# Two changes to the order of issue in a selective-scan and spectral-convolution kernel: decays two scans ahead, product copies 500 columns later

## The chip, the cores and the metric

The kernel runs on one core of one Trainium2 chip. The metric is the device time of one execution in microseconds. Five engines work side by side, each through its own queue in order: TensorE (PE in the profile, its weight loads PEld), VectorE (DVE), ScalarE (ACT), GpSimd (POOL) and SyncE (SP), which here only issues DMAs. They meet through semaphores.

## The reference

The input is a batch of four images of 48 × 48 tokens with 128 channels. Layer 0 is a selective scan over the image in four directions, layer 1 self-attention and then a spectral convolution:

```python
# layer 0: group norm, projection, 3x3 depthwise convolution, SiLU; then for 4 directions k
x_dbl = einsum('bkdl,kcd->bkcl', xs, x_proj_w)          # -> dts_r, B, C
dt = softplus(einsum('bkrl,kdr->bkdl', dts_r, dt_proj_w) + dt_proj_b)
h = h * exp(dt_l[..., None] * A) + (dt_l * u_l)[..., None] * B_l   # 2304 steps, 256 x 16 states
y = einsum('bkdn,bkn->bkd', h, C_l)
# the four directions are added, normed, gated and projected; x = x + that
# layer 1: t = t + softmax(ln(t) ln(t)^T) ln(t)
# then, with u = ln(t), for prefixes of 1, 1/2, 1/4 and 1/8 of the tokens:
U_plus  = causal convolution of u with 16 filters
U_minus = the same with alternating signs
out = einsum('btkd,k,kde->bte', U_plus, s, Mpp) + einsum('btkd,k,kde->bte', U_minus, s, Mpm)
out = out + three shifted products of u with M_u
# t = t + weighted sum of the four prefixes' outputs
```

All is computed in float32.

## The kernel before, in words

Each image goes through a prologue (norm, projection, convolution), the scans, an epilogue with attention, and the spectral convolution, which the code calls `stu`. The scans of image b share their time with other work for TensorE: for image 0 with the mixing of the filter matrices (`mixture`), for images 1 to 3 with the `stu` of image b − 1. The `stu` of the last image runs alone at the end.

**The scans.** A chunk is one direction and 384 tokens; there are 24 chunks an image. A chunk has 8 units (two halves of the channels by four groups of states), and a unit four scans, so an image has 768 scans. For each unit VectorE, or GpSimd for three units in eight, multiplies dt·u by B (L451, `enter`); for each scan ScalarE computes the decay exp(dt·A) (L458) into one of three PSUM banks `dAs`, and VectorE runs the scan (L461). GpSimd multiplies the states by C (L470) and keeps the last state (`carry`, L469), TensorE adds over the states (L478), and VectorE adds the result to the image's sum (L484). The first decay of a unit is preceded by a small copy of the carried state into the unit's first column (L456).

**The other ScalarE work of these stages.** `spread` copies a row of B into a PSUM bank for VectorE's multiply (L443). The preparation of a later chunk, cut into small steps by `prepare`, copies projections out of PSUM (L375, L385) and computes a Softplus (L393)[...].

**The Toeplitz products.** `stu` walks through 80 items an image: five blocks of output columns, four of them 126 wide and the last 72, by 16 filters. Each item has three products c = 0, 2, 1 of shifted filters with u (L992), then two projections (L1051, L1055) for the item two before it. The product c = 0 is copied to a second bank (L1006, cy from cx); c = 2 adds to the first bank and c = 1 to the second; both are then copied to `U` (L1011 and L1012, L1009). Each bank has one buffer. A copy isn't issued right behind its product: `later` puts it on a list, and it is issued once so many columns of later matmuls have been issued:

```python
        def later(f):
            late.append([LATER, f])
```

Only the first entry of the list is counted down (`do_late`), and a matmul of a block of width w has two columns for each of its output tokens: 252 or so in the wide blocks, 144 in the last.

**The order.** It is written out by hand and each engine follows it. For every unit s, `scans` goes through enter, a step of preparation, scan 0, a share of TensorE's other work (`more`), the multiply by C of the unit before, scan 1, the addition of a finished y, a step of preparation, `more`, `spread` for unit s + 2, scan 2, `more`, a step of preparation, scan 3, the loads of B and C for the next chunk, the sum over states of unit s − 2, and `more`. `more` takes from the other work so many matmuls that both pieces of work end together; the copies it is due are issued on ScalarE in the same place. In this order a scan's decay is issued immediately ahead of its scan.

SP issues the loads of filters (tt), chunk inputs (rep, bc) and small matrices (G) in the same written order.

Of the kernel before, what the change touches and what calls it, by code (L numbers as in the profile page):

```python
# [24 lines left out]
G4, DL, C4, Q4 = 4, 32, 4, 4  # L25
# [10 lines left out]

BLOCKS = [(0, 126, 0, 72), (126, 252, 1, 18), (252, 378, 2, 36), (378, 504, 3, 0), (504, 576, 3, 0)]
SHIFT = 55.0
LATER = 300


class Stage:
# [13 lines left out]
def hybrid_kernel(ctx: ExitStack, tc: tile.TileContext, a: dict, out: bass.AP):  # L56
# [375 lines left out]
    class Unit:  # L432
# [17 lines left out]
            eng = nc.gpsimd if self.pool else nc.vector  # L450
            eng.tensor_tensor(s, self.ch.rep[self.h][:, :, 1], bt.unsqueeze(1).to_broadcast([P, G4, CS]), ALU.mult)  # L451

        def scan(self, g, i, dAs):
            ch = self.ch
            if g == 0:
                nc.scalar.copy(self.full[:, :, ch.slot], none if ch.first else carry[:, self.h, self.q])  # L456
            dA = dAs[(G4 * i + g) % len(dAs)]
            nc.scalar.activation(dA[:, 1:CS + 1], ch.rep[self.h][:, g, 0], AF.Exp,  # L458
                                 scale=A[:, ch.k, self.h * G4 + g, self.q:self.q + 1])
            s = self.full.rearrange("p g t -> p (g t)")[:, ch.scanned(g)]  # L460
            nc.vector.tensor_tensor_scan(s, dA[:, CS + 1:0:-1] if ch.rev else dA[:, :CS + 1], s, 0.0,  # L461
                                         ALU.mult, ALU.add)
# [49 lines left out]
    def scans(b, chunks, preps, front, sp, back, work, work_cols):  # L512

        units = [Unit(ch, h, q) for ch in chunks for h, q in quads]
        total = len(chunks) * CHUNK_COLS + work_cols
        done = [0]

        def more(share):

            while done[0] < share * total:  # L520
                cols = next(work, None)
                if cols is None:
                    break
                done[0] += cols

        def enter(s):

            if s + 2 < len(units) and units[s + 2].pool:
                units[s + 2].enter(sp.s)
            if 0 <= s + 1 < len(units) and not units[s + 1].pool:  # L530
                units[s + 1].enter(sp.s)

        def spread(s):
            if s < len(units) and not units[s].pool:
                units[s].spread(back.psB)

        def prepare(s):

            ci, j = divmod(s, len(quads))
            for c in range(ci + 1, ci + 4):  # L540
                if c < len(chunks) and 0 <= s - len(quads) * c + LEAD < STEPS:
                    done[0] += next(preps[c]) or 0

        def refill(s, i):

            if 0 <= s < len(units) and s // len(quads) + 1 < len(chunks):
                u, nxt = units[s], chunks[s // len(quads) + 1]
                if u.h == NH - 1:
                    nxt.fetch(i + u.q, front)

        pending = []
        dAs = [back.psa.tile([P, 512], F32, tag=f"dA{i}", name=f"dA{b}_{i}") for i in range(3)]
        for t in dAs:
            nc.vector.memset(t[:, 0:CS + 2:CS + 1], 0.0)
        spread(0)
        enter(-2)
        enter(-1)
        spread(1)
        for s in range(len(units) + 2):
            real = s < len(units)  # L560
            enter(s)
            prepare(s)
            if real:
                units[s].scan(0, s, dAs)
            more((s + 0.25) / len(units))
            if 1 <= s <= len(units):
                units[s - 1].times_c()
            if real:
                units[s].scan(1, s, dAs)
            if pending:  # L570
                pending.pop().add_y()
            prepare(s)
            more((s + 0.5) / len(units))
            spread(s + 2)
            if real:
                units[s].scan(2, s, dAs)
            more((s + 0.75) / len(units))
            prepare(s)
            if real:
                units[s].scan(3, s, dAs)  # L580
            refill(s - 3, Q4)
            refill(s + 1, 0)
            if s >= 2:
                units[s - 2].sum_c(back.psy)
                done[0] += CS
                if units[s - 2].q == Q4 - 1:
                    pending.append(units[s - 2])
            more((s + 1) / len(units))
        for u in pending:
            u.add_y()  # L590
        assert next(work, None) is None
# [308 lines left out]
    def stu(b, pool, ps, seeds):  # L900
# [22 lines left out]
        def do_late(cols=None):  # L923

            if cols is not None and late:
                late[0][0] -= cols
            while late and (cols is None or late[0][0] <= 0):
                late.pop(0)[1]()

        def later(f):  # L930
            late.append([LATER, f])

# [39 lines left out]
        def conv(n, c):  # L972

            assert seq.pop(0) == (n, c)
            (lo, hi, place, extra), k = items[n]
            w = hi - lo
            v = w + (c != 1)
            t = tts[n, c]
            if c == 0:
                banks[0] = ps.psc.tile([P, 512], F32, tag="x", name=f"cx{b}_{n}")  # L980
            elif 1 not in banks:
                do_late()
            p = banks.pop(1) if c == 1 else banks[0]
            p4 = p[:, :4 * v].rearrange("p (e m) -> p e m", e=4)
            nb = (hi + P - 1) // P
            for g in range(2):
                first = lo - (g == 1 and c != 1)
                for J in range(nb):
                    at = max(first, J * P) if J else first
                    end = J * P - 1  # L990
                    x = (sums[:, J, g], u[:, J, 2 + g], u[:, J, g])[c]
                    nc.tensor.matmul(p4[:, 2 * g:2 * g + 2, v - (hi - at):], x,  # L992
                                     t[:, :, hi - 1 - at + J * P:end if end >= 0 else None:-1],
                                     start=(c == 0 and J == 0 and g == 0), stop=(J == nb - 1 and g == 1),
                                     skip_group_check=(c > 0))
                    do_late(2 * (hi - at))
                    if g == 1 and J == nb - 1:
                        later(lambda: taken(n, c, p, w))
                    yield 2 * (hi - at)

        def taken(n, c, p, w):
            if c == 0:
                U[n] = pool.three.tile([P, 8 * P], F32, tag="U", name=f"U{b}_{n}")[:, :8 * w].rearrange(
                    "p (c g e m) -> p c g e m", c=2, g=2, e=2)
                banks[1] = ps.psc.tile([P, 512], F32, tag="y", name=f"cy{b}_{n}")
                nc.scalar.copy(banks[1][:, :4 * w].rearrange("p (e m) -> p e m", e=4),  # L1006
                               p[:, :4 * (w + 1)].rearrange("p (e m) -> p e m", e=4)[:, :, 1:])
            elif c == 1:
                nc.scalar.copy(U[n][:, 0].rearrange("p g e m -> p (g e m)"), p[:, :4 * w])  # L1009
            else:  # L1010
                nc.scalar.copy(U[n][:, 1, 0], p[:, :2 * (w + 1)].rearrange("p (e m) -> p e m", e=2)[:, :, 1:])  # L1011
                nc.scalar.copy(U[n][:, 1, 1].rearrange("p e m -> p (e m)"), p[:, 2 * w + 3:4 * w + 3])  # L1012
# [71 lines left out]
        for n, (_, k) in enumerate(items):  # L1084
            if k == 0:
                begin(n)
            yield from conv(n, 0)
            fetch()
            if n > 0:
                fetch_G(n - 1)  # L1090
            if n > 1:
                if k == 2:
                    yield from ar(n - 2)
                yield from project(n - 2)
            for c in (2, 1):
                yield from conv(n, c)
                fetch()
            if n > 1 and k == 1:
                do_late()
                yield from end(n - 2)  # L1100
# [50 lines left out]
    for b in range(B):  # L1151
# [3 lines left out]
        if b == 0:  # L1155
            mixed = Stage(tc, "m", "right", two=(2, SB))
            scans(b, *first, front, sp, ps, mixture(mixed, ps), MIX_COLS)
            mixed.close()
        else:
            scans(b, *first, front, sp, ps, stu_alone(b - 1, ps, 1), STU_COLS)  # L1160
# [99 lines left out]
```

## Time and profile before

| | |
|---|---|
| median of 3 runs | 6137.34 us (6124.15 to 6143.45) |
| profiled execution | 6131.63 us |
| its span | 6129.9 us |
| PE busy, share | 5042.3 us, 82% |
| PE weight loads | 3316.1 us, 54% |
| DVE | 4264.0 us, 70% |
| ACT | 3258.1 us, 53% |
| POOL | 3630.6 us, 59% |
| scans L461 | 3072, 942 ns each |
| decays L458 | 3072, 584 ns each |
| copies L1011 | 320, 349 ns each |

An engine is busy while it computes; time in which it waits for a semaphore is not counted, and where the profile can tell, it names the instruction that ended the wait, the releaser. TensorE's matmuls are pipelined and their ends are modelled, so its busy time is less sharp than that of the others. The times of single rows come from this one execution. The chain of waits that ended last is made of PE 43%, DVE 25%, DMA 11% and ACT 10%.

### The profile page before, as it was taken

The page shows a single profiled execution, that of the slowest core. Times are in us where ns is not written, and L with a number is a line of the kernel's source. Part 1 is how long each engine was busy: PE and PEld are TensorE (multiplying, and loading weights), DVE is VectorE, ACT ScalarE, POOL GpSimd, SP SyncE. Part 2 cuts the span into 40 slices and gives each one's busy share as a digit, 9 for nine tenths or more (in the row PEclk, how much of TensorE's full clock was granted, in tenths as well). Part 3 has the DMA queues.
Part 4 walks back from the last instruction along what each step waited for, and adds up shares of the span by engine and source line. Part 5 has one row for each costly group of instructions (what it writes and reads, how often), then busy time and mean ns, then how long its engine had stood idle before and what let it go on. Part 6 is the DMA issues. An engine that isn't in the chain of part 4 may idle for free.

```text
span 6129.9 us, 76036 instructions
## 1 busy us (share of the span) xinstructions
PE 5042.3 (82%) x24850; PEld 3316.1 (54%) x24850; DVE 4264.0 (70%) x4926; ACT 3258.1 (53%) x6909; POOL 3630.6 (59%) x1823
## 2 busy tenths in 40 slices
PE   3555555797889988788889988888889998889999
PEld 1111111445556667545556666535556666558889
DVE  6999999458888998458888898448889998210000
ACT  2666666246666665247666665247666665232111
POOL 1988889307788888207788888108778887100000
PEclk6777777799999999899999999889999999899999
DMA  3445444117767777117767777027777776035546
GB/s 109 157 147 165 156 157 159 33 65 205 215 209 244 234 248 250 38 65 223 210 216 238 234 245 247 30 79 220 210 222 236 233 251 228 7 87 156 159 141 208
DMA packets 734954, 1062.79 MB, mean 173 GB/s; under 512 B 158272, under 2 KB 543424, under 8 KB 734528
## 3 DMA queue, kind: packets, MB, share of 16 engines
q1 hardware_dynamic: 728736, 1054.63, 54.6%
q10 hardware_dynamic: 5824, 3.30, 0.3%
q8 instruction: 199, 3.26, 0.2%
q14 instruction: 195, 1.60, 0.1%
HBM read 939.60 MB, written 117.98 MB: 173 GB/s over the span
## 4 chain that ended last, share of the span: by engine, by line
PE 43%; DVE 25%; DMA 11%; ACT 10%; SPq 5%; issue 4%; POOL 2%; ACTq 0%; DVEq 0%; POOLq 0%
PE cx L992 13%; DVE s L461 12%; PE cy L992 6%; DVE s L451 6%; DMA rep<-dtdud 4%; PE s L718 4%; PE y L478 3%; PE o L711 3%; ACT dA L458 3%; SPq L430 3%; DMA bc<-xdd 3%; PE pr L1055 2%; DMA tt<-fd 2%; PE pr L1051 2%; PE op L654 2%
## 5 line engine op out<-in xcount | busy, mean ns | idle before, releaser
L461 DVE TENSOR_TENSOR_SCAN s<-dA,s 128x385 f32<-128x385 f32 x3072 | 2735.4, 942 | 496.5 <-ACT dA L458 494.2
L470 POOL TENSOR_TENSOR s<-s,bc 128x1536 f32<-128x1536 f32 x768 | 2440.1, 3178 | 171.7 <-DVE s L461 95.0
L458 ACT ACTIVATE dA<-rep,A 128x384 f32<-128x384 f32 x3072 | 1747.2, 584 | 504.0 <-DVE s L461 471.2
L451 POOL TENSOR_TENSOR s<-rep,bc 128x1536 f32<-128x1536 f32 x288 | 993.4, 3449 | 90.6 <-DMA bc<-xdd 90.6
L478 PE MATMUL y<-s,csum 128*32 128x384 f32 x6144 | 723.9, 546 | 239.7 <-DVE ya L484 154.6
L992 PE MATMUL cx<-tt,u 128*128 128x254 f32 (+7 forms) x3840 | 830.8, 361 | 83.6 <-DMA tt<-fd 49.2
L992 PE MATMUL cx<-tt,us 128*128 128x254 f32 (+7 forms) x3840 | 809.5, 353 | 52.3 <-ACT U L1012 24.9
L451 DVE TENSOR_TENSOR s<-rep,B 128x1536 f32<-128x1536 f32 x480 | 830.4, 1730 | 14.2 <-ACT B L443 14.2
L992 PEld LDWEIGHTS cx<-tt,u 128*128 128x128 f32 x3840 | 653.5, 197 | 279.9 <-issue 132.9
L992 PE MATMUL cy<-tt,u 128*128 128x252 f32 (+5 forms) x3840 | 787.1, 348 | 0.0
L992 PEld LDWEIGHTS cx<-tt,us 128*128 128x128 f32 x3840 | 641.2, 191 | 240.3 <-issue 82.8
L992 PEld LDWEIGHTS cy<-tt,u 128*128 128x128 f32 x3840 | 639.8, 190 | 146.2 <-issue 85.9
L1079 DVE TENSOR_TENSOR res<-res,ot 126x512 f32<-126x512 f32 (+1 forms) x20 | 13.4, 671 | 686.5 <-PE ot L1073 686.1
L478 PEld LDWEIGHTS y<-s,csum 128*32 128x32 f32 x6144 | 128.3, 112 | 589.8 <-issue 375.5
L469 POOL COPY carry<-s 128x4 f32<-128x4 f32 x640 | 121.6, 190 | 535.2 <-DVE s L461 523.5
L1011 ACT COPY U<-cx 128x252 f32<-128x252 f32 (+1 forms) x320 | 111.8, 349 | 597.3 <-PE cx L992 594.4
L834 PE MATMUL G<-M,W 128*128 128x256 f32 (+3 forms) x512 | 255.5, 620 | 174.6 <-DMA M<-in_M_phi_plus 92.7
L720 ACT ACTIVATE e<-s,shift 128x512 f32<-128x512 f32 (+1 forms) x360 | 231.1, 644 | 312.8 <-PE s L718 312.2
L718 PE MATMUL s<-xnT 128*128 128x512 f32 (+1 forms) x720 | 355.8, 579 | 42.9 <-ACT xnT L680 23.6
L156 POOL TENSOR_TENSOR ln_vu<-ln_vu,mhalf 128x4 f32<-128x4 f32 (+1 forms) x20 | 26.8, 1342 | 603.5 <-DVE ln_vu L155 603.5
L443 ACT COPY B<-bc 128x384 f32<-128x384 f32 x480 | 229.9, 479 | 251.8 <-DVE s L451 222.8
L1055 PEld LDWEIGHTS pr<-U,G 128*128 128x128 f32 x2048 | 304.4, 191 | 102.8 <-issue 78.6
(165 smaller groups left out, 4951.7 us busy)
## 6 DMA issues: line engine op xcount, KB each, us to landing
rep<-dtdud SPq DMA_DIRECT2D x768, 384.0 KB, 5.2
bc<-xdd SPq DMA_DIRECT2D x3072, 48.0 KB, 3.2
tt<-fd SPq DMA_DIRECT2D x192, 577.0 KB, 4.2
tt<-fd SPq DMA_DIRECT2D x192, 505.0 KB, 4.4
dtdud<-re SPq DMA_DIRECT2D x192, 384.0 KB, 4.2
tt<-fd SPq DMA_DIRECT2D x192, 379.0 KB, 3.5
G<-gd SPq DMA_DIRECT2D x192, 256.0 KB, 5.4
tt<-fd SPq DMA_DIRECT2D x64, 506.0 KB, 5.5
```

Source lines behind the costliest of these rows:

```text
L430: nc.sync.dma_start(t[c::C4], src[row].partition_broadcast(DL))
L443: nc.scalar.copy(self.bt[:, :CS], self.ch.bc[self.q])
L451: eng.tensor_tensor(s, self.ch.rep[self.h][:, :, 1], bt.unsqueeze(1).to_broadcast([P, G4, CS]), ALU.mult)
L458: nc.scalar.activation(dA[:, 1:CS + 1], ch.rep[self.h][:, g, 0], AF.Exp, scale=A[:, ch.k, self.h * G4 + g, self.q:self.q + 1])
L461: nc.vector.tensor_tensor_scan(s, dA[:, CS + 1:0:-1] if ch.rev else dA[:, :CS + 1], s, 0.0, ALU.mult, ALU.add)
L470: nc.gpsimd.tensor_tensor(self.s, self.s, ch.bc[Q4 + self.q].unsqueeze(1).to_broadcast([P, G4, CS]), ALU.mult)
L478: nc.tensor.matmul(ch.y[g * DL:(g + 1) * DL, :CS], csum, self.s[:, g], start=(self.q == 0), stop=(self.q == Q4 - 1))
L718: nc.tensor.matmul(p[:, :w], xnT[:, i * P:(i + 1) * P], xnT[:, 512 * J:512 * J + w], start=True, stop=True)
L720: nc.scalar.activation(e[:, :w], p[:, :w], AF.Exp, bias=shift)
L834: nc.tensor.matmul(p[:, :n], W[:, q if t else 0, i], M[t][:, i].unsqueeze(1).to_broadcast([P, n, C]), start=(t == 0 and i == 0), stop=(t = ...
L992: nc.tensor.matmul(p4[:, 2 * g:2 * g + 2, v - (hi - at):], x, t[:, :, hi - 1 - at + J * P:end if end >= 0 else None:-1], start=(c == 0 and ...
L1055: nc.tensor.matmul(p[:, 1 - g, :, v0:v1], G, U[n][:, ::-1 if g else 1, g, 1, v0:v1], start=False, stop=(k == KF - 1 and g == 1 and v1 == w))
```

## The change

Two things change, and nothing is added to or taken from what is computed.

First, the decay and the small copy of the carried state leave `Unit.scan` for a method of their own, `Unit.decay`. Ahead of the loop the first two decays are issued. From then on, immediately ahead of scan i, the decay of scan i + 2 is issued, into the bank that scan i − 1 read. The three banks remain three.

Second, `LATER` is 500 in place of 300, and at the end of each item's last product (c = 1) the list of copies is first counted down by another 500 columns.

```diff
-LATER = 300
+LATER = 500
...
-        def scan(self, g, i, dAs):
+        def decay(self, g, dA):
             ch = self.ch
             if g == 0:
                 nc.scalar.copy(self.full[:, :, ch.slot], none if ch.first else carry[:, self.h, self.q])
-            dA = dAs[(G4 * i + g) % len(dAs)]
             nc.scalar.activation(dA[:, 1:CS + 1], ch.rep[self.h][:, g, 0], AF.Exp,
                                  scale=A[:, ch.k, self.h * G4 + g, self.q:self.q + 1])
+
+        def scan(self, g, dA):
+            ch = self.ch
             s = self.full.rearrange("p g t -> p (g t)")[:, ch.scanned(g)]
             nc.vector.tensor_tensor_scan(s, dA[:, CS + 1:0:-1] if ch.rev else dA[:, :CS + 1], s, 0.0,
                                          ALU.mult, ALU.add)
...
+        def decay(i):
+            if i < G4 * len(units):
+                units[i // G4].decay(i % G4, dAs[i % len(dAs)])
+
+        def scan(s, g):
+            i = G4 * s + g
+            decay(i + len(dAs) - 1)
+            units[s].scan(g, dAs[i % len(dAs)])
...
+        for i in range(len(dAs) - 1):
+            decay(i)
         for s in range(len(units) + 2):
...
             if real:
-                units[s].scan(0, s, dAs)
+                scan(s, 0)
...
                     if g == 1 and J == nb - 1:
+                        do_late(LATER if c == 1 else 0)
                         later(lambda: taken(n, c, p, w))
```

The scans 1, 2 and 3 of a unit are called in the same way as scan 0.

More of the change, by code (lines that the diff above doesn't have):

```diff
@@ L568, in scans @@
             if real:
-                units[s].scan(1, s, dAs)
+                scan(s, 1)
             if pending:
@@ L575, in scans @@
             if real:
-                units[s].scan(2, s, dAs)
+                scan(s, 2)
             more((s + 0.75) / len(units))
@@ L579, in scans @@
             if real:
-                units[s].scan(3, s, dAs)
+                scan(s, 3)
             refill(s - 3, Q4)
```

## The prediction

> **What bounds the kernel now.** I read the page's busy shares first, then busy times per stage, then who waited for whom in one stage, then the order of time. The table by stretches (columns: stretch and its length, busy of PE, PE weight loads, DVE, ACT and POOL in us, granted clock, DMA share, GB/s) for the four scan stages, one per image, and for the tail in which TensorE works alone:
>
> ```profile
> 122.80:1099.50 976.70, 535.72 (x2160) 171.61 (x2160) 911.67 (x977) 643.45 (x1356) 872.73 (x423) 0.72 0.48 156
> 1398.00:2462.00 1064.00, 948.04 (x5368) 659.02 (x5372) 922.23 (x983) 694.97 (x1521) 872.91 (x422) 0.97 0.74 231
> 2760.00:3827.00 1067.00, 951.40 (x5368) 662.93 (x5369) 923.05 (x983) 694.71 (x1521) 873.07 (x422) 0.96 0.73 230
> 4125.00:5198.00 1073.00, 954.05 (x5368) 664.58 (x5372) 923.14 (x983) 694.39 (x1521) 873.13 (x423) 0.96 0.73 229
> 5455.00:6125.00 670.00, 667.96 (x3690) 597.59 (x3688) 2.75 (x4) 133.45 (x318) 0.00 (x0) 1.00 0.54 165
> ```
>
> The scan stages hold 4181 of 6130 us. In the first, VectorE is the fullest (93%) and TensorE half idle. In the other three TensorE (89%), VectorE (87%) and GpSimd (82%) are all nearly full and none is full: they lose time waiting for each other. The tail is TensorE alone, at 99.7%. The waits over the span say through whom:
>
> ```profile
> ACT U L1011 <- PE cx L992: 594.4, 237, 7.9
> ...
> DVE s L461 <- ACT dA L458: 494.2, 360, 10.2
> ACT dA L458 <- DVE s L461: 471.2, 596, 2.9
> ```
>
> In the scan stages VectorE's idle time has practically one cause: a scan whose decay ScalarE has not written (494 us: 62.4, 140.7, 142.6 and 148.5 in the four). ScalarE is not short of time (65% busy); it stands at a copy of a Toeplitz product that TensorE has not finished. In order of time (columns: start, us, engine, line, operation, count, idle before and its releaser):
>
> ```profile
> 2108.56 0.56 ACT L1006 COPY cy<-cx 128x504 f32<-128x504 f32 x1 [1.85 <-PE cx L992]
> ...
> 2109.03 0.49 ACT L443 COPY B<-bc 128x384 f32<-128x384 f32 x1
> ...
> 2109.44 1.09 ACT L458 ACTIVATE dA<-rep,A 128x384 f32<-128x384 f32 x2
> 2110.07 1.81 DVE L461 TENSOR_TENSOR_SCAN s<-dA,s 128x385 f32<-128x385 f32 x2 [1.58 <-ACT dA L458]
> ```
>
> ScalarE waits 1.85 us for the product, copies, and only then writes the decay; the scan waits 1.58 us. TensorE's own waits in 1398 to 2462 (us, times, longest):
>
> ```profile
> PE cx L992 <- DMA tt<-fd: 26.8, 11, 7.8
> PE xp L370 <- DVE s L451: 23.9, 8, 5.0
> PE y L478 <- DVE ya L484: 19.3, 11, 2.8
> PE dt L382 <- DVE s L451: 11.0, 18, 1.1
> PE cx L992 <- ACT U L1012: 8.0, 6, 3.7
> PE cx L992 <- ACT cy L1006: 5.4, 6, 1.8
> ```
>
> So TensorE holds ScalarE, ScalarE holds VectorE, and VectorE, late, holds TensorE (54 us a stage: 23.9 + 19.3 + 11.0).
>
> **What the skill says.** The Trainium skill, "PSUM — Partial Sum Buffer", Engine vs sequencer instructions: ScalarE's queue is strictly first in, first out. The trace agrees: in the lines above the decays stand behind the waiting copy although their own buffers were free. "ScalarE: Activation LUTs", What ACT_TABLE_LOAD costs: a load of 1283 ns plus some 1380 ns of drain. The trace shows the 1283 ns (89 loads on line 458, 95 on 393), but no drain of that size: a load from 2111.66 is followed by its Softplus at 2112.96. "Perfetto Trace Analysis", Identifying the Most-Contended Engine: judge TensorE's headroom by weight-load share, not by matmul busy time. Here weight loads fill 62% of the mixed stage against 89% of the tail, so the 89% "busy" overstates TensorE. The same Toeplitz matmuls (line 992) are busy 600 us (2880) in the stage and 530 us (2858) in the tail; 530 × 2880/2858 / 0.97 for the clock is 551, so about 49 us of the busy time is stall.
>
> **Part 1: decays ahead.** Nothing is added or removed: 3072 Exps (584 ns), 768 slot copies (about 0.19 us) and 3072 scans remain, with no DMA among what moves. With three decay buffers the decay of scan i+2 is issued just ahead of scan i, so it waits for scan i-1; before, the decay of scan i waited for scan i-3. Buffers, and so decays in flight, are as before. What changes is where the rest of ScalarE's queue (product copies, B copies, xd, re, Softplus) stands: two scans later against VectorE.
>
> Gain to VectorE: when ScalarE stands at something, two scans are already fed. Four scans in one row take 3.51 us, two take 1.81 us: cover of 1.8 us. I took the idle before each scan in three stretches of 100 us (1500, 2100, 2900): 30 waits, 41.9 us; what exceeds 1.8 us in them sums to 4.6 us. Cover could take away 89% of VectorE's waiting, if nothing else came next.
>
> TensorE comes next. If all its waits on VectorE and ScalarE went, a mixed stage would hold its 948 busy plus about 42 of other waits (26.8 and 3.5 of DMA, 4.7 issue, 4.1 POOL, 2.9 residual): 990. With the 49 of stall inside "busy" gone too: 941. VectorE's floor is 1064 − 141 = 923. So the ceiling is 74 to 123 us a stage. I take the part that follows directly: VectorE up to 1.8 us earlier ends the y waits (19.3; 11 of 1.75) and dt waits (11.0), and of the 8 xp waits of 3.0 us 1.8 each (14): 44 us. The waits on ScalarE and DMA I leave. 3 × 44 = 132.
>
> First stage: TensorE has room, so VectorE decides. Once per chunk (24) ScalarE does table load 1.28, Softplus 0.85, B copy 0.48, table load 1.28 and decay 0.58; two such places show 2.63 and 0.87 us of scan idle. Afterwards the decay ahead of Softplus ends 0.58 after a scan's end, Softplus 2.13 later (2.7), while two scans last 1.8: the product L409 then waits 0.9, and the second load hides under it (1.5 us). So 24 × 0.9 = 22 us stay, and of the longest wait, 10.2, some 8.4: 62 − 22 − 8 = 32, taken as 30.
>
> What is queued behind the decay's longer wait: copies to cy (TensorE's next product into the same bank needs it about 1.0 us later, after the second projection), copies to U (the next cx), xd and re (dt products), dtdud's store. While TensorE is the late one, these are ready to run when the product ends; the decay before them was done during ScalarE's idle time. B copies, which waited 62.5 us in the first stage and some 51 in the second for VectorE's multiply L451, no longer wait: the decays now ahead of them already need a scan after that multiply.
>
> **Part 2: 500 columns.** Followed through the block widths (252 or so per matmul in the first four blocks, 144 in the last): two matmuls of the wide blocks give 500 to 506, and 300 also needed two. Only the last block moves: 14 to 16 copies each of two kinds per image, plus two others, one matmul later. The forced flush at the end of each third product finds nothing left. A 144-column matmul takes 0.14 us (12 in 1.72), so 3 × 33 × 0.14 = 14 us of ScalarE waiting at most, gained or (if TensorE then waits) lost. I take 0: about 830 columns (0.8 us) remain before the bank is needed, the two copies take 0.54. In the tail TensorE is full and ScalarE idle: 0.
>
> Sum: 132 + 30 = 162. The profiled execution took 6131.6 us (span 6129.9), giving 5970; the median of the runs shown lies 5.7 above it: **5975 us**.
>
> **Rivals.** *Larger:* the loop opens wholly and stages go to 960–990: 3 × (74 to 110) plus 30 gives 250 to 360 less, 5780–5890. For: weight-load share and the stall inside "busy". Against: [...]DMA is at 74%.
> *TensorE bound:* VectorE's idle moves from scans to elsewhere, TensorE's waits on VectorE are replaced by waits for tt loads (26.8 already) and ScalarE. Then only the first stage and crumbs: 25 to 80 less, 6057–6112.
> *Copies late (slower):* a copy now waits for scan i-2 instead of i-4. Where TensorE runs ahead of VectorE, cx waits at cy and U copies. In 1450 to 2350 some 66 items had 42 U and 34 cy copies that waited for TensorE; 56 had no wait. If those end 1.8 us later with 1.0 us of slack, TensorE loses 0.8 × 56 = 45 us in 900, 53 a stage, 160 in all; less the first stage's 30, about +130, 6265, and +20 where half of it comes. It decides once TensorE is more than two scans plus 1 us ahead of VectorE. Against: ScalarE waited for TensorE at most copies, so TensorE is behind.
> *Nothing:* gain and loss cancel, 6120–6155.
>
> **Chances.** Forecast case (80 to 230 less, 5905–6057) 0.58; larger 0.10; TensorE bound 0.13; nothing 0.05; slower 0.14. Range: 5830 to 6125 holds the forecast, the TensorE-bound case, most of the larger one and a little of nothing: about 0.8. The forecast's own range is 5905–6057. Faster by over 0.3% (about what a measurement here can tell from no change) 0.81, within 0.05, slower 0.14.
>
> **What would show it.** Right: scan idle put down to decays falls from 494 to 150–300; ScalarE's wait for scans (471) grows, its waits for cx and cy shrink; B copies' wait for L451 vanishes; mixed stages 1010–1030 us, first stage about 945; tail unchanged near 670. New small waits of L409 on Softplus. Wrong: cx waits on U or cy copies above 60 us a stage (copies late), or mixed stages still at 1050 with waits for tt loads grown (TensorE bound).

## The result and the profile after

The changed kernel takes 5962.09 us (median of 4 runs, 5960.9 to 5963.57) against 6138.39 us before (median of 4 runs, one more than in the table ahead of the prediction): a ratio of 0.9717, 95% interval 0.97 to 0.9733. The forecast was 5975. The span of the profiled execution is 5961.6 us, 168.3 less than the 6129.9 before.

The table by stretches of the kernel after (stretch and length, busy of PE, PE weight loads, DVE, ACT, POOL, granted clock, DMA share, GB/s), cut again at the first and last scan of each image, with the tail last:

```profile
122.30:1105.20 982.90, 519.85 (x2160) 165.12 (x2160) 911.44 (x977) 646.25 (x1356) 872.66 (x423) 0.72 0.48 155
1405.30:2416.60 1011.30, 935.48 (x5368) 656.74 (x5372) 924.27 (x983) 698.80 (x1519) 871.96 (x422) 0.98 0.77 243
2716.00:3725.00 1009.00, 935.12 (x5368) 657.46 (x5370) 924.16 (x983) 699.09 (x1519) 872.06 (x422) 0.98 0.78 244
4023.20:5027.80 1004.60, 933.42 (x5368) 656.27 (x5372) 924.02 (x983) 698.83 (x1519) 871.92 (x422) 0.98 0.77 244
5285.00:5955.00 670.00, 667.68 (x3686) 597.12 (x3685) 2.75 (x4) 133.73 (x319) 0.00 (x0) 1.00 0.54 165
```

The three mixed stages are shorter by 52.7, 58.0 and 68.4 us, together 179. The first stage is 6.2 us longer. The busy times of VectorE and GpSimd are what they were; only their waiting went. TensorE's busy time fell too, by 12.6, 16.3 and 20.6 us, while its granted clock rose from 0.97, 0.96 and 0.96 to 0.98. Lines have moved: scan L461 is L463, decay L458 is L457, the product L992 is L1005, the copies L1006 and L1011 are L1020 and L1025. The waits over the span (us, times, longest):

```profile
ACT dA L457 <- DVE s L463: 702.6, 892, 4.0
...
ACT U L1025 <- PE cx L1005: 512.1, 224, 7.0
...
DVE re L409 <- ACT re L393: 192.3, 96, 20.3
...
DVE s L463 <- ACT dA L457: 97.3, 92, 9.7
```

Scans waited 494 us for their decays before and wait 97 now, while decays wait 703 for scans instead of 471. A wait of 192 us is new in size (55.5 before, none of that within the scans): VectorE's product L409 behind Softplus. VectorE's longest waits in 1405.3 to 2416.6, where before there were 140.7 us for decays and 0.6 for all else:

```profile
DVE re L409 <- ACT re L393: 30.5, 22, 2.8
DVE s L463 <- ACT dA L457: 27.7, 29, 4.5
DVE ya L486 <- PE y L480: 13.2, 9, 3.9
```

In order of time, with the rows of ScalarE and VectorE alone, a product copy late as before:

```profile
2103.77 1.64 ACT L457 ACTIVATE dA<-rep,A 128x384 f32<-128x384 f32 x3
2104.72 1.72 DVE L451 TENSOR_TENSOR s<-rep,B 128x1536 f32<-128x1536 f32 x1
2106.36 5.19 DVE L463 TENSOR_TENSOR_SCAN s<-dA,s 128x385 f32<-128x385 f32 x6
2106.87 0.56 ACT L1020 COPY cy<-cx 128x504 f32<-128x504 f32 x1 [1.46 <-PE cx L1005]
2107.35 0.59 ACT L457 ACTIVATE dA<-rep,A 128x384 f32<-128x384 f32 x1
```

ScalarE again stands 1.46 us before the copy, most of it while VectorE multiplies (L451). The six scans then run without a gap: the decays of the first three already lie in the three banks (the row of three), and ScalarE goes on with the fourth at 2107.35, when the second scan has hardly begun. TensorE's own waits in 1405.3 to 2416.6, to be held against those of 1398 to 2462 before:

```profile
PE cx L1005 <- DMA tt<-fd: 38.1, 13, 6.2
PE cx L1005 <- ACT cy L1020: 10.8, 11, 1.6
PE pr L1065 <- DMA G<-gd: 7.7, 4, 4.1
PE y L480 <- POOL s L472: 6.7, 5, 4.4
PE cx L1005 <- ACT U L1026: 5.5, 5, 1.9
...
PE dt L382 <- DVE s L451: 3.4, 8, 0.5
PE xp L370 <- DVE s L451: 2.2, 2, 1.7
PE y L480 <- DVE ya L486: 0.7, 2, 0.4
```

Its waits on VectorE fell from 54.2 to 6.3 us. Its waits for filter loads rose from 26.8 to 38.1.

### The profile page after: what moved, and what is told of

It is laid out like the page before. It is cut to its first block, busy times and chain, and to the rows that moved or that the text cites. A ratio compares the mean times of both kernels' runs of the same rounds, so it can differ in the third digit from the quotient of the medians.

```text
span 5961.6 us, 76285 instructions
## 1 busy us (share of the span) xinstructions
PE 4979.4 (84%) x24850; PEld 3293.9 (55%) x24850; DVE 4268.3 (72%) x4926; ACT 3276.5 (55%) x6909; POOL 3627.4 (61%) x1823
## 4 chain that ended last, share of the span: by engine, by line
PE 44%; DVE 19%; DMA 16%; ACT 7%; SPq 6%; issue 4%; POOL 3%; ACTq 0%; DVEq 0%; POOLq 0%
PE cx L1005 14%; DVE s L463 9%; PE cy L1005 7%; DMA rep<-dtdud 6%; PE s L731 4%; DVE s L451 4%; PE o L724 3%; DMA tt<-fd 3%; PE y L480 3%; SPq L430 3%; DMA bc<-xdd 3%; PE pr L1069 3%; DMA G<-gd 2%; PE pr L1065 2%; PE op L667 2%
## 5 line engine op out<-in xcount | busy, mean ns | idle before, releaser
L463 DVE TENSOR_TENSOR_SCAN s<-dA,s 128x385 f32<-128x385 f32 x3072 | 2702.0, 938 | 100.0 <-ACT dA L457 97.3
L472 POOL TENSOR_TENSOR s<-s,bc 128x1536 f32<-128x1536 f32 x768 | 2440.3, 3180 | 190.6 <-DMA bc<-xdd 78.4
L457 ACT ACTIVATE dA<-rep,A 128x384 f32<-128x384 f32 x3072 | 1752.8, 584 | 746.4 <-DVE s L463 702.6
L451 POOL TENSOR_TENSOR s<-rep,bc 128x1536 f32<-128x1536 f32 x288 | 993.8, 3451 | 94.2 <-DMA bc<-xdd 93.1
L1005 PE MATMUL cx<-tt,u 128*128 128x254 f32 (+7 forms) x3840 | 819.4, 357 | 110.9 <-DMA tt<-fd 65.7
L451 DVE TENSOR_TENSOR s<-rep,B 128x1536 f32<-128x1536 f32 x480 | 831.1, 1732 | 56.0 <-ACT B L443 26.0
L1005 PE MATMUL cx<-tt,us 128*128 128x254 f32 (+7 forms) x3840 | 809.8, 353 | 59.4 <-DMA tt<-fd 34.5
L1005 PEld LDWEIGHTS cx<-tt,u 128*128 128x128 f32 x3840 | 642.9, 194 | 306.5 <-issue 103.1
L1005 PE MATMUL cy<-tt,u 128*128 128x252 f32 (+5 forms) x3840 | 785.3, 347 | 0.0
L1005 PEld LDWEIGHTS cx<-tt,us 128*128 128x128 f32 x3840 | 641.4, 191 | 247.8 <-issue 81.7
L1005 PEld LDWEIGHTS cy<-tt,u 128*128 128x128 f32 x3840 | 638.0, 189 | 144.9 <-issue 85.1
L1093 DVE TENSOR_TENSOR res<-res,ot 126x512 f32<-126x512 f32 (+1 forms) x20 | 13.4, 668 | 694.5 <-PE ot L1087 694.5
L847 PE MATMUL G<-M,W 128*128 128x256 f32 (+3 forms) x512 | 244.6, 595 | 240.9 <-DMA M<-in_M_phi_plus 118.9
L1025 ACT COPY U<-cx 128x252 f32<-128x252 f32 (+1 forms) x320 | 111.5, 349 | 512.5 <-PE cx L1005 512.1
L156 POOL TENSOR_TENSOR ln_vu<-ln_vu,mhalf 128x4 f32<-128x4 f32 (+1 forms) x20 | 26.8, 1341 | 602.0 <-DVE ln_vu L155 602.0
L1069 PE MATMUL pr<-U,G 128*128 128x144 f32 (+6 forms) x2048 | 348.9, 308 | 0.0
L724 PE MATMUL o<-e,xn 128*128 128x512 f32 (+1 forms) x720 | 343.6, 560 | 4.5 <-ACT e L733 4.5
```

The source lines that it names most:

```text
L472: nc.gpsimd.tensor_tensor(self.s, self.s, ch.bc[Q4 + self.q].unsqueeze(1).to_broadcast([P, G4, CS]), ALU.mult)
L724: nc.tensor.matmul(po[J][:, :w], xn[:, i], e[:, :w], start=(i == 0), stop=(i == NT - 1))
L847: nc.tensor.matmul(p[:, :n], W[:, q if t else 0, i], M[t][:, i].unsqueeze(1).to_broadcast([P, n, C]), start=(t == 0 and i == 0), stop=(t = ...
L1069: nc.tensor.matmul(p[:, 1 - g, :, v0:v1], G, U[n][:, ::-1 if g else 1, g, 1, v0:v1], start=False, stop=(k == KF - 1 and g == 1 and v1 == w))
```

## The experiments

**Each part alone.** The first takes part 2 out of the change, the second makes part 2 alone:

```diff
-LATER = 500
+LATER = 300
...
-                        do_late(LATER if c == 1 else 0)
```

> Decays two scans ahead, copies due after 300 columns as before. Theory (the decays carry all of the gain): within 10 us of the changed kernel's 5962, mixed stages 1005 to 1015 us. Rival (the later copies free ScalarE in the last block): 10 to 30 us above it.

Measured: 5970.64 us, ratio 0.9739 (0.9725 to 0.9754); mixed stages 1007, 1010 and 1015 us, where the whole change has 1011, 1009 and 1005.

> Copies due after 500 columns and the countdown at the third product, decays immediately ahead of their scans as before. Theory: within 10 us of the 6138 before, since only copies of the last block of 72 columns move, by one matmul of 0.14 us. Rival: 10 to 30 us faster, all of it in the last 222 us of each mixed stage.

Measured: 6134.88 us, ratio 1.0002 (0.9996 to 1.0009). The later copies do nothing by themselves, and the decays carry the gain. The first run's ratio lies 0.0022 above that of the full change, with intervals that overlap, so a few microseconds of interplay can't be excluded. Single stages differ by up to 10 us between that run's profile and the full change's, one way and the other: a stage of one profile can be off by so much.

**One scan ahead.** The second scan of lead taken away, all else as changed:

```diff
-            decay(i + len(dAs) - 1)
+            decay(i + 1)
...
-        for i in range(len(dAs) - 1):
+        for i in range(1):
```

> Decays one scan ahead instead of two, three buffers still, copies after 500 columns. Cover theory: one scan of 0.9 us covers, of the 30 waits looked at before (41.9 us), about 25 us; the caps give 60 percent of VectorE's gain, so some 100 of the 175 us: about 6035. Rival (the position of ScalarE's other work matters, not the cover): half of the gain or less, or no difference between one and two.

Measured: 5954.01 us, ratio 0.9711 (0.9696 to 0.9725): as good as two ahead. What the cover theory said of the scans' waits came true: 59.2 us of 140.7 are left in the first mixed stage, 58% gone where 60 were foreseen. What falls is its step from these waits to the time. The stages are 960.2, 1008.7, 1007.5 and 1014.6 us. VectorE's waits in 1405 to 2416 of this kernel:

```profile
DVE s L463 <- ACT dA L457: 59.2, 69, 2.9
DVE ya L486 <- PE y L480: 10.2, 3, 5.0
DVE re L409 <- ACT re L393: 6.3, 8, 1.2
```

With two ahead the scans wait 27.7 us in such a stage and L409 30.5, together 58; with one ahead 59.2 and 6.3, together 66. The second scan of lead moves the wait from the scans to L409: Softplus now stands behind a decay that waits for a later scan, and VectorE meets L409 before Softplus is done. In the trace, the decays among the five ScalarE instructions ahead of each Softplus waited 15.6 us for scans in this stage with two ahead, and 1.5 us with one.

**The first image undone.** Two ahead for images 1 to 3, the old order in the first stage:

```diff
-            decay(i + len(dAs) - 1)
+            decay(i + (len(dAs) - 1 if b else 0))
...
-        for i in range(len(dAs) - 1):
+        for i in range(len(dAs) - 1 if b else 0):
```

> Decays two ahead for images 1 to 3 alone; in the first image's stage, which mixes the filter matrices, immediately ahead of their scans as before. Theory (in the first stage the change only moved the waiting, through TensorE's later wait for copies of G): first stage 977 us as before, the others 1005 to 1015; total 0 to 8 us below the changed kernel. Rival (the first stage's length differs by chance of one profile): total equal or up to 5 us above.

Measured: 5960.41 us, ratio 0.9725 (0.9711 to 0.974); first stage 975.7 us, as before. The totals can't settle 7 us, but the stages of six profiles do: 982.9, 982.4 and 981.9 us with two ahead (the change, the decays alone, and the kernel with less for TensorE below), 976.7, 976.7 and 975.7 with none (before, the copies alone, and this one). So the change as made gains nothing there and costs some 6 us. VectorE's waits in the first stage of this kernel (122 to 1099) and, in the second fence, of the changed kernel (122 to 1100):

```profile
DVE s L463 <- ACT dA L457: 61.9, 44, 11.1
DVE ya L486 <- PE y L480: 2.8, 2, 2.0
```

```profile
DVE re L409 <- ACT re L393: 25.2, 22, 1.9
DVE ya L486 <- PE y L480: 21.7, 10, 3.6
DVE s L463 <- ACT dA L457: 17.4, 9, 9.7
```

The scans' 62 us became 17, and 44 us came back as L409 behind Softplus and as the sum `ya` behind TensorE's y. TensorE is late there because its filter mixing waits. Of the ten waits of `ya`, six (9.6 us) follow a matmul of the mixing, G, that stood at ScalarE, at a copy of G (Gm) or at a decay; three (10.2 us) follow a G that stood at a load of M. G behind Gm rose from 48.4 us in the undone kernel to 80.9 in the changed one, G behind loads of M from 79.5 to 118.9. SP issues these loads behind the stores of G, which wait for ScalarE too: 98.1 us undone, 125.3 changed. That this is why the loads came later is argued, not shown. With one ahead this stage was 960.2 us (and 961 in each of the two later kernels that have one ahead there): there is something to gain here, and two ahead goes past it.

**Is TensorE the bound now?**

The kernel leaves out the second projection's matmuls in the mixed stages, so for images 0 to 2:

```diff
...
-                    for g in range(2):
+                    for g in range(2 if b == B - 1 else 0):
```

> The changed kernel with the second projection's 512 matmuls (L1069) of each spectral convolution inside the mixed stages left out, for images 0 to 2: their results are incomplete. These matmuls are busy some 86 us a stage. If TensorE bounds the mixed stages: 50 to 80 us shorter each (down to about 940). If VectorE's waits for Softplus and the order do: 0 to 20 us. If the DMAs do: 0, with waits for tt and bc unchanged.

Measured: 5972.47 us, ratio 0.9738 (0.9712 to 0.9764). The first mixed stage of this kernel, and TensorE's longest wait in it:

```profile
1403.70:2408.40 1004.70, 887.83 (x4855) 596.96 (x4855) 926.09 (x983) 699.87 (x1519) 871.00 (x422) 0.95 0.78 245
```

```profile
PE cx L1005 <- DMA tt<-fd: 54.1, 22, 5.8
```

TensorE's busy time in the stage is 48 us less (935.5 to 887.8), not the 86 us or so of the removed rows, because the rest took longer at a lower granted clock: the Toeplitz products 618 us in place of 597, at 0.95 in place of 0.98. So the kernel took away half of what was meant. Still, the three stages are 1004.7, 1007.0 and 1014.3 us. VectorE's waits in the first of them are as they were (28.2 us for L409, 26.7 for scans), and TensorE's room turned into waiting. TensorE's busy time does not bound the mixed stages after the change.

**Moving L409 out of Softplus's way.** Two kernels issued it one step later, with two ahead and with one:

```diff
+            yield
             for h in range(NH):
                 x = in_order(xc[h], k, self.lo, CS)
...
                 nc.vector.tensor_tensor(dx, dt, x, ALU.mult)
             yield
-            yield
             store(0)
```

> The changed kernel with VectorE's product dt times x (L409) issued one preparation step later, that is after the next unit's multiply instead of right behind Softplus. Theory (with decays two ahead the second scan of cover is paid back where VectorE meets L409 and waits for Softplus, 192 us over the span with the prologue, about 25 to 31 us a stage): L409's waits in the stages nearly vanish; each stage 10 to 25 us shorter, 5890 to 5930. Rival (TensorE or the DMAs bound the mixed stages near 1008): waits move to scans, ya or bc, mixed stages within 5 us of 1008, only the first stage gains, 5945 to 5965.

> Decays one ahead and L409 one preparation step later. Theory: with one ahead L409 hardly waited (6 us a stage), so 0 to 5 us a stage from the one-ahead kernel, 5935 to 5955. Rival (the later product itself helps by giving scans room behind the table load): 5 to 15 us a stage.

Measured: with two ahead 6227.66 us, ratio 1.0152 (1.0136 to 1.0168), with one 6465.67 us, ratio 1.0541 (1.0525 to 1.0557). Both expectations missed by far, and neither theory had the reason. L409 (L410 in this kernel) no longer waits before it starts, but it takes longer; its group with two ahead (count, busy and mean ns, idle before), and a piece of the order of time of VectorE and GpSimd:

```profile
L410 DVE TENSOR_TENSOR re<-re,xc 128x384 f32<-128x384 f32 x192 | 440.8, 2335 | 10.1 <-ACT re L393 10.1
```

```profile
2020.66 3.17 POOL L472 TENSOR_TENSOR s<-s,bc 128x1536 f32<-128x1536 f32 x1 [1.25 <-DVE s L463]
2021.15 1.75 DVE L451 TENSOR_TENSOR s<-rep,B 128x1536 f32<-128x1536 f32 x1 [0.64 <-ACT B L443]
2022.83 5.14 DVE L410 TENSOR_TENSOR re<-re,xc 128x384 f32<-128x384 f32 x2
2023.79 3.76 POOL L451 TENSOR_TENSOR s<-rep,bc 128x1536 f32<-128x1536 f32 x1
```

In the changed kernel L409 takes 800 ns on average. Here two of them take 5.14 us: the first starts while GpSimd's L472 runs to 2023.83, the second ends only after GpSimd's next multiply, at 2027.55. VectorE's multiply L451, which reads B from PSUM, is not slowed in the same company (1.75 us; 1.73 on average in the changed kernel). The Trainium skill, "SBUF — State Buffer", Who interferes with whom, says that a VectorE instruction with two SBUF inputs contends with a GpSimd instruction that reads SBUF, through ports that they share and that only one holds at a time. L409 has two SBUF inputs, and the trace agrees: in the kernel with two ahead, the 162 of its 192 that run beside a GpSimd instruction take 2649 ns on average, the other 30 take 638. In the changed kernel only 35 have such company (1297 ns), and 157 have not (689). So these runs say nothing on Softplus; they measured the price of a new place.

**A fourth decay buffer,** placed in SBUF, while the three others stay in PSUM:

```diff
-            decay(i + len(dAs) - 1)
+            decay(i + 2)
...
+        dAs.append(sp.d.tile([P, CS + 2], F32, tag="dA3", name=f"dA{b}_3"))
...
```

> Decays two ahead, but four decay buffers (the fourth in SBUF): the decay of scan i+2 waits for scan i-2 instead of i-1, so that ScalarE's other work stands as it does with one ahead while the cover is two scans. Theory (position of the other work against VectorE is what costs with two ahead): L409 waits fall to the 6 us a stage of one ahead, scan waits stay near 27: stages 10 to 25 us shorter than the changed kernel. Rival (mixed stages are bound elsewhere at 1008): mixed stages within 5 us of it.

Measured: 6471.77 us, ratio 1.0554 (1.0536 to 1.0572). The scans' group in this kernel:

```profile
L463 DVE TENSOR_TENSOR_SCAN s<-dA,s 128x385 f32<-128x385 f32 x3072 | 3516.8, 1204 | 25.0 <-ACT dA L457 24.8
```

The waits for decays are nearly gone (25 us over the span) and the scans themselves take 1204 ns on average instead of 938; the longest takes 3839. One scan in four reads its decay from SBUF, and it alone is slower: in the trace these 768 take 2013 ns on average, the other 2304 take 934, though most of those run beside GpSimd as well. Of the 768, 525 take over 1.1 us, each beside a GpSimd instruction; of the other 243, 218 have none beside them. One of the slow ones, and its company:

```profile
159.60 3.30 DVE L463 TENSOR_TENSOR_SCAN s<-dA,s 128x385 f32<-128x385 f32 x1
```

```profile
158.92 3.17 POOL L472 TENSOR_TENSOR s<-s,bc 128x1536 f32<-128x1536 f32 x1
```

This fits the same page, since such a scan has two SBUF inputs. The experiment could not tell apart what it was made for.

**Softplus earlier.** The other way round, which leaves L409 in its place:

```diff
             yield from rest()
-            yield
-
             nc.scalar.activation(re[:, :, 0], re[:, :, 0], AF.Softplus)
+            yield
             yield 0
```

> The changed kernel with Softplus issued one preparation step earlier on ScalarE, ahead of the unit's first scan; VectorE's product L409 stays where it was, away from GpSimd's multiplies. Theory (two ahead pays back its second scan in L409's wait for Softplus): L409 waits fall from 25 to 31 us a stage to under 8, its duration stays near 0.8 us; stages 10 to 25 us shorter, 5870 to 5930. Rival (VectorE's idle time only changes its name, because ScalarE's chain of two table loads has to fit somewhere): scans take over the wait and stages stay within 5 us, 5950 to 5970.

Measured: 5953.93 us, ratio 0.9702 (0.9688 to 0.9717); stages 974, 1005, 1011 and 1009 us. VectorE's first waits in 1450 to 2350 of this kernel; L409 has none left:

```profile
DVE s L463 <- ACT dA L457: 49.2, 40, 4.0
DVE ya L486 <- PE y L480: 8.4, 7, 2.6
```

In the changed kernel the same stretch had 19.8 for scans and 29.1 for L409, together 48.9. The rival held: the wait changed its name and kept its size.

> Decays one ahead and Softplus one preparation step earlier. Theory: L409 hardly waited with one ahead, so 0 to 5 us a stage, 5930 to 5960; more cover would have to come from two ahead, and then the Softplus-earlier kernel with two ahead is the faster of the two. Rival: equal effect in both.

Measured: 5980.76 us, ratio 0.9741 (0.9723 to 0.9759); mixed stages 1021, 1019 and 1028 us, 12 to 13 us longer than with one ahead alone. Of the two kernels with Softplus earlier, that with two ahead is the faster, by 27 us: here the second scan of cover is worth something. Why one ahead loses by an earlier Softplus the runs don't show. That it would be the faster was expected; the 0 to 5 us a stage against one ahead alone were a miss.

**No table switch.** ScalarE computes Softplus and Exp from different tables. In the changed kernel a load of 1.28 us stands ahead of 95 of the 96 Softplus and of 89 decays, and none ahead of the copies, which run with either table. This kernel puts Exp in Softplus's place, so its values are others, and neither line has a load left:

```diff
-            nc.scalar.activation(re[:, :, 0], re[:, :, 0], AF.Softplus)
+            nc.scalar.activation(re[:, :, 0], re[:, :, 0], AF.Exp)
```

> The changed kernel with Exp computed where Softplus stands (L393), so that ScalarE needs no table switch within the scans: other values, the same shapes and order. Theory (what is left of VectorE's waiting in a mixed stage, some 60 us for scans and L409, is mostly the two table loads of 1.28 us in each of 24 chunks, 62 us a stage): L409 and scan waits together fall from 58 to under 25 us, stages 20 to 45 us shorter, 5790 to 5890. Rival (GpSimd, TensorE and the DMAs at over 85 percent each would hold the stage): waits move to bc, ya and tt, stages within 10 us, 5920 to 5965.

Measured: 5938.41 us, ratio 0.9681 (0.9664 to 0.9699). The first stage fell to 964.8 us, the mixed ones are 1007.9, 998.5 and 1006.8. In 1450 to 2350, L409's wait fell from 29.1 to 3.2 us, but scans wait 27.5 (19.8 with the table loads), and GpSimd waits longer for its rows of C:

```profile
POOL s L472 <- DMA bc<-xdd: 34.2, 19, 3.5
```

It was 27.2. VectorE's busy time in the first mixed stage grew from 924 to 939 us, as L409's mean rose to 1081 ns over the span: 58 of its 192 now ran beside a GpSimd instruction and took 2004 ns. Two table loads of 1.28 us in each of 24 chunks are 62 us of ScalarE a stage, and taking them out gave 3, 10 and −2 us in the mixed stages, no more than single profiles differ by; in the first stage the loads were worth 18. The rival's number held in the mixed stages, but not for its reason alone: VectorE's idle time fell by 18, 23 and 12 us there, and 12 to 15 us of that went into the longer L409. So this kernel doesn't show what the loads would be worth without that contention.

**The best of it together:** one ahead in the first stage, two ahead and Softplus earlier in the others.

```diff
-            yield
-
+            if not self.b:
+                yield
             nc.scalar.activation(re[:, :, 0], re[:, :, 0], AF.Softplus)
+            if self.b:
+                yield
             yield 0
...
-            decay(i + len(dAs) - 1)
+            decay(i + (len(dAs) - 1 if b else 1))
...
-        for i in range(len(dAs) - 1):
+        for i in range(len(dAs) - 1 if b else 1):
```

> Decays one ahead in the first image's stage, two ahead in the others, Softplus one step earlier in those. Theory (stages add up independently): first stage 960 as with one ahead, the others 1005 to 1011 as with Softplus earlier: 5935 to 5945. Rival (within the spread of runs of the one-ahead kernel): 5945 to 5960.

Measured: 5945.4 us, ratio 0.9696 (0.968 to 0.9712), on the border of the two expectations. Its interval overlaps those of the changed kernel and of one ahead, so it is the lowest of the kernels that compute everything, and not shown to be better.

## Why the prediction was right, and where it was not

*The loop, right.* The forecast said that TensorE holds ScalarE, ScalarE VectorE and VectorE TensorE, and that the lead opens this loop. The decays alone gave the gain, the scans' waiting fell by 397 us, and TensorE's waits on VectorE fell by 48, 51 and 51 us in the mixed stages where 44 were taken for each.

*The mixed stages, right with a term left out.* 132 us were forecast for the three and 179 came. In the stage compared above, 53 us went: 48 of TensorE's waits on VectorE and 12.6 of its busy time (948.0 to 935.5), less 15.5 more of waits for tt and G loads and 2.6 more for GpSimd; what remains is in small rows. So the term of the sum was near (132 us, where the waits on VectorE gave 150 in the three stages), and what the sum lacked is TensorE's shorter busy time, another 49 us in the three. The forecast had worked out 49 us a stage of stall inside "busy" and left them out of its sum, but it isn't these that came back: the Toeplitz products, from which it took them, were busy 600 us before and 597 after. The busy time fell by 1.3, 1.7 and 2.2%, about as much as the granted clock rose (0.967 to 0.979, 0.962 to 0.979 and 0.959 to 0.982: 1.3, 1.7 and 2.4%). The forecast had no term for a changed clock.

*The first stage, wrong.* The step "TensorE has room, so VectorE decides", with 30 us of gain, failed: the stage was 6 us longer, and 975.7 when undone. The 0.9 us foreseen for L409 behind Softplus, 22 us, was right (25.2). What the step left out is that TensorE, though half idle, was late in places: G waited 33 us longer for ScalarE's copies and 26 us longer for loads of M, and VectorE's `ya` waited 19 us longer for y. This is the "copies late" rival in the main, priced for the mixed stages only, and it came in the other one.

*Size of the cover, right for the waits and not for the time.* The 1.8 us of cover and the 89% came near for the scans' waits (140.7 to 27.7 us in the stage compared, 80%), but not for the time: one scan ahead gave the same. The second scan was worth 27 us only where Softplus was moved as well. That it is the place of ScalarE's other work, and no longer the length of the lead, that counts in the mixed stages is argued from this.

*Part 2, right.* Zero was forecast and 1.0002 measured.

*The rivals.* "Larger" (stages of 960 to 990) did not come. "TensorE bound" did not come either: it foresaw mixed stages of 1050, and after the change 48 us less of TensorE's busy time moved nothing. Its sign, longer waits for tt loads, did show. "Copies late" stayed small in the mixed stages: cy and U copies held TensorE 16.3 us, against 13.4 before. Of the signs named, scan waits went below the 150 to 300 foreseen, the B copies' wait for L451 fell from 222.8 to 7.3 us, and the tail stayed at 670; two of the three mixed stages ended below the 1010 to 1030 foreseen, and the first stage at 983 instead of 945.

*Open.* What holds the mixed stages near 1008 us is not settled. One or two ahead, 48 us less of TensorE's busy time, Softplus earlier with two ahead, and no table loads all left them between 998 and 1015, the last with a slower L409 in place of the loads. VectorE is at 91%, GpSimd at 86%, and the waits that grow when something else goes are those for loads (tt, G, bc) at a DMA share of 0.77. That the loads are the next bound is argued from this, and no run lightened them.

## What to carry to other kernels

In a queue that runs in order, look for what stands between a producer and its consumer: ahead of a wait for a third engine, a lead of one item may be all that is needed, and a longer one can move the same wait to whatever else the queue feeds. Price the lead for every consumer of that queue in each stage, also for an engine that is half idle, because it can still be late. And before an instruction is moved, see what GpSimd is doing at the new place, if it is VectorE's and reads two inputs from SBUF.

## What had not been expected of the hardware

VectorE instructions with both inputs in SBUF were stretched by GpSimd's 3.2 to 3.5 us multiplies: L409 from 0.80 to 2.34 us on average by moving it one step, and scans from 0.93 to 2.01 us by moving their decays from PSUM to SBUF. One decay in four outside PSUM cost 510 us (6472 against 5962), some three times what the change gained.

TensorE's granted clock went, roughly, with its busy share. In the first mixed stage of six kernels TensorE was busy 85, 86, 88, 89, 90 and 92.5% of the time, and the clock was 0.93, 0.94, 0.95, 0.97, 0.96 and 0.98 (one ahead with L409 later, four buffers, less for TensorE, before, two ahead with L409 later, after); in the first stage before it was 55% and 0.72, in the tail 99.7% and 1.00. Which of the two leads isn't shown. In the changed kernel the gain so came twice, as less waiting and as shorter matmuls; and where work was taken from TensorE, some 86 us of rows went but only 48 us of busy time.
